# Reordering the start of a graph-network kernel: the first group's third gather, its b pieces and layer 1's bias columns

## The chip, the core and the metric

The kernel runs on one core of a Trainium2 chip. A core has five engines that each work through their own queue of instructions in order: TensorE (PE, matrix products; its weight loads are shown apart as PEld), VectorE (DVE), ScalarE (ACT), GpSimd (POOL) and SyncE (SP, which here only issues DMAs). An instruction that needs the result of another engine waits for a semaphore, and everything behind it in its own queue waits with it. The metric is the device time of one execution in microseconds.

## The reference

Two layers work on 128 graphs of 128 nodes with 64 features. `adj` is a random weighted adjacency matrix; about an eighth of the entries are positive, the first nodes of a graph much more than the last.

```python
# layer 0
mask = (adj > 0.0)
h = relu((x @ W1a)[:, :, None, :] + (x[:, :, None, :] - x[:, None, :, :]) @ W1b + b1)   # 192 wide, per pair j, k
hm = einsum('bjkh,bjk->bjh', h, mask)
x = layernorm(x + hm @ W2 + mask.sum(-1)[..., None] * b2)
# layer 1
m = relu(relu(x @ g_W1 + g_b1) @ g_W2 + g_b2)
msg = relu(adj @ m)
x = layernorm(x + gru(msg @ W_ih.T + b_ih, x @ W_hh.T + b_hh, x))
```

For a pair (j, k) the argument of the relu is u[j] + v[k], with u and v linear in x. The sum over a node's neighbours of relu(u + v) is half of the sum of u + v plus half of the sum of |u + v|. The first half is linear; the kernel gets the second by gathering the v of each node's neighbours, adding u, and summing absolute values.

## The kernel before, in words

The graphs go through in 32 groups of four (`G = 4`). For one group:

- `load`: adjacency, transposed features and features by DMA.
- `masks` (L411, POOL): the mask of all four graphs. `ranks` (L418 PE, L421 ACT) number each node's neighbours; `turned` (L483 PE, L486 ACT) transposes these ranks. `degrees` (L426 PE, L429 and L431 DVE) count neighbours, `counts` (L436 to L446, six small POOL instructions) derive from them how many extra places the nodes need. `offsets` (L453 PE, L456 ACT, L463 and L464 DVE, L470 POOL) and `places` (L500, L504, L507 PE, L510 ACT) lay out those extra places.
- `values0`, `values1` (L527, L530 PE, L534 ACT): u and v of two graphs each. The copy L534 puts them into the tile `uv`. The second matmul (L530) adds bias rows from the tile `three`.
- `pieces`: v is split into three bf16 parts b0, b1, b2, whose sum is v. In group 0 this is done graph by graph: cast (L546 ACT), remainder r (L549 DVE), cast (L552 ACT), remainder (L555 POOL). In later groups it is done for four graphs at once, with r on POOL.
- `picks` (L517, DVE): one-hot matrices, from the ranks (`pick0`, eight) or from the places (`pick1`, four).
- Per graph, four stretches over `pick0` and two over `pick1`. A stretch has a `seed` (L580, ACT: u is copied into a PSUM tile `pv`, of which there are three), a `gather` (L611, PE: 12 matmuls that add the picked b0, b1 and b2) and a `reduce` (L627, DVE: absolute values summed into `part`). The stretches of `pick1` take their u from `us`, which `over` (L591 PE, L598 ACT) computes from `own32`, the output of L470.
- `together`, `sums`, `second` and the rest: the parts are added up and go through layer 1.

The order is written out by hand. Each part is a generator that yields between its steps, and a table gives each step a time; the steps of all groups are sorted by time, and each engine's queue gets its instructions in that order. The times order the steps and do nothing else. Group g's step of time t stands at `g * 768 + t`. Group 0 has a table of its own for its beginning, `FIRST`, with one entry per step; `SETUP` does the same for the preparation of constants. Steps of one time keep the order in which the table names the parts.

```python
for t in SETUP:
    plan.setdefault(t, []).append(run)
...
        if g == 0 and name in FIRST:
            times = FIRST[name] + times[len(FIRST[name]) :]
        run = parts[name]()
        for t in times:
            plan.setdefault(g * PER + t, []).append(run)
...
    for t in sorted(plan):
        for run in plan[t]:
            next(run, None)
```

The last step of `SETUP` prepares layer 1's bias columns on DVE (L242, L243, L245, then L151, L153 or L155 and L160 from `three_rows`, which splits a row of biases into three bf16 rows): 11 instructions that end in the columns of `three` from 256 on. Layer 1 of group 0 reads them first, in L313. The steps around it are group 1's `masks` at 768 - 559 = 209 and its `degrees` at 768 - 402 = 366 and 768 - 367 = 401.

Of the kernel before, what the change touches and what calls it, by code (L numbers as in the profile page):

```python
# [47 lines left out]
}  # L48


SETUP = (-8001, -7999, -7610, -7530, -7400, -7380, -700, -690)
FIRST = {
    "load": (-8000, -7998), "masks": (-7580,), "ranks": (-7520, -7515), "degrees": (-7389, -7388), "counts": (-7387,),
    "offsets": (-7372, -7371, -7366, -7366, -7366, -7366, -7365), "turned": (-7359, -7358),
    "values0": (-7375, -7374, -7370), "values1": (-7368, -7364, -7360), "pieces": (-7373, -7363, -7355, -7350),
    "places": (-7357, -7356), "pick0": (-7512, -7512, -7512, -7512, -7365, -7365, -7365, -7365),
    "pick1": (-7352, -7352, -7351, -7351), "over0": (-7349, -7348), "seed": (-7369, -7366, -7361, -7354),
    "gather": (-7367, -7362, -7354, -7351), "reduce": (-7365, -7358, -7353, -7350),
}


# [18 lines left out]
def adj_resnorm_kernel(  # L80
# [299 lines left out]
    with ExitStack() as fast:  # L380
# [316 lines left out]
        name, g, run = "setup", -1, setup(ps_g, ps_w)  # L697
        for t in SETUP:
            plan.setdefault(t, []).append(run)
# [141 lines left out]
```

## Time and profile before

| what | us |
|---|---|
| median of 3 runs (1056.05 to 1056.41) | 1056.37 |
| the profiled execution | 1053.67 |
| its span | 1051.9 |
| DVE busy | 968.2 |
| PE busy | 952.7 |
| ACT busy | 943.2 |
| POOL busy | 883.3 |

The span runs from the first to the last instruction; the profiled execution's own time is 1.8 us longer. A row of the timeline gives start, duration, engine, line, operation, output and inputs; where the engine was idle just before, brackets give for how long and what ended the wait. In a row with xN, N instructions are merged. The chain of waits goes back from the last instruction, at each step to what released it or to the instruction ahead of it on its engine.

### The profile page before, as it was taken

What the parts mean: (1) busy time and instruction counts of PE and PEld (TensorE: products, weight loads), DVE (VectorE), ACT (ScalarE), POOL (GpSimd) and SP (SyncE); (2) the same over time, 40 slices, a digit from 0 to 9 for tenths busy, and PEclk for the clock granted to TensorE, in tenths of its full rate; (3) what the DMA queues carried; (4) which work ended last, traced back from release to release, by engine and by line L of the source; (5) the groups of instructions that cost most, each with busy time, mean ns of one, the idle gap of its engine ahead of it and who ended that gap; (6) DMA issues with size and microseconds to landing.
All of it is one profiled execution on the core that took longest, in us unless ns stands there. A gap on an engine that the chain in (4) does not pass through costs nothing.

```text
span 1051.9 us, 33435 instructions
## 1 busy us (share of the span) xinstructions
PE 952.7 (91%) x13432; PEld 762.5 (72%) x13432; DVE 968.2 (92%) x2192; ACT 943.2 (90%) x1608; POOL 883.3 (84%) x1291
## 2 busy tenths in 40 slices
PE   6798999999999999999999999999999999999983
PEld 4577777777777777777777777777777877777762
DVE  6888999999999999999999999999999999999971
ACT  4789999999999999999999999999999999999861
POOL 2568788889889888988888898988898888889765
PEclk9799999999999999999999999999999999999995
DMA  4000000000000000000001000000000000000000
GB/s 110 1 22 2 22 22 22 27 27 13 16 27 27 28 27 26 3 27 27 27 27 27 22 7 27 26 27 27 27 4 25 27 27 27 26 7 7 2 7 27
DMA packets 21368, 23.95 MB, mean 23 GB/s; under 512 B 4050, under 2 KB 17112, under 8 KB 21208
## 3 DMA queue, kind: packets, MB, share of 16 engines
q1 hardware_dynamic: 21208, 21.76, 7.1%
q8 instruction: 107, 1.75, 0.7%
q14 instruction: 53, 0.43, 0.1%
HBM read 17.55 MB, written 4.19 MB: 21 GB/s over the span
## 4 chain that ended last, share of the span: by engine, by line
POOL 37%; DVE 29%; ACT 14%; PE 12%; issue 8%; DMA 0%; SPq 0%; POOLq 0%; DVEq 0%; ACTq 0%
DVE part L627 15%; ACT pv L580 7%; POOL part L649 6%; POOL part L653 4%; POOL part L656 4%; PE pv L611 4%; DVE pick L517 4%; POOL r L549 4%; POOL part L651 4%; POOL b L555 3%; DVE own L464 3%; DVE stats L269 2%; POOL yc L279 2%; POOL ua L360 2%; POOL rs L276 2%
## 5 line engine op out<-in xcount | busy, mean ns | idle before, releaser
L627 DVE TENSOR_REDUCE part<-pv 128x192 f32<-128x768 f32 x768 | 699.3, 948 | 32.0 <-PE pv L611 17.5
L611 PE MATMUL pv<-b,pick 64*128 64x192 bf16 x9216 | 501.9, 244 | 39.0 <-ACT pv L580 34.9
L611 PEld LDWEIGHTS <-pick 64*128 64x128 bf16 x9216 | 385.4, 94 | 123.6 <-issue 94.1
L580 ACT COPY pv<-uv 128x768 f32<-128x768 f32 x512 | 407.5, 804 | 16.8 <-DVE part L627 14.5
L580 ACT COPY pv<-us 128x768 f32<-128x768 f32 x256 | 204.6, 817 | 13.2 <-DVE part L627 13.1
L649 POOL TENSOR_TENSOR part<-part 128x384 f32<-128x384 f32 x128 | 127.9, 999 | 19.1 <-DVE part L627 17.3
L534 ACT COPY uv<-pu 128x512 f32<-128x512 f32 x128 | 75.1, 587 | 27.7 <-PE pu L530 23.5
L527 PE MATMUL pu<-wall,xT 64*128 64x512 f32 x256 | 92.0, 637 | 1.6 <-ACT off L456 1.2
L517 DVE TENSOR_SCALAR pick<-rankT 128x512 bf16<-128x512 bf16 x256 | 88.7, 367 | 1.5 <-ACT rankT L421 1.5
L669 PE MATMUL ph<-ownT,part 128*96 128x128 f32 x512 | 87.6, 273 | 0.2 <-POOL part L656 0.2
L470 POOL CAST own<-own 128x512 f32<-128x512 bf16 x32 | 19.6, 611 | 75.2 <-DVE own L464 69.1
L651 POOL TENSOR_TENSOR part<-part 128x192 f32<-128x192 f32 x128 | 77.5, 605 | 5.1
L555 POOL TENSOR_TENSOR b<-r,b 128x1024 bf16<-128x1024 f32 (+1 forms) x35 | 68.9, 1968 | 11.8 <-ACT b L552 8.5
L653 POOL TENSOR_TENSOR part<-part 128x192 f32<-128x192 f32 x128 | 75.9, 593 | 2.6
L591 PE MATMUL pz<-uv,own 128*128 128x192 f32 x256 | 58.6, 352 | 20.4 <-DVE n L352 12.0
L656 POOL TENSOR_TENSOR part<-part 128x192 f32<-128x192 f32 x128 | 75.8, 592 | 0.0
L288 PE MATMUL pw<-w2c,hmT 96*128 96x64 f32 x512 | 75.1, 278 | 0.5 <-ACT hmT L675 0.5
L288 PEld LDWEIGHTS pw<-w2c,hmT 96*128 96x128 f32 x512 | 69.7, 191 | 6.6 <-issue 4.9
L669 PEld LDWEIGHTS ph<-ownT,part 128*96 128x96 f32 x512 | 70.8, 165 | 1.8 <-POOL part L656 0.7
L668 PE MATMUL ph<-ident,part 128*96 128x128 f32 x256 | 71.0, 277 | 0.8 <-POOL part L653 0.6
L276 POOL TENSOR_TENSOR rs<-ve,nhalf 128x4 f32<-128x4 f32 x64 | 66.6, 1040 | 5.3
L549 POOL TENSOR_TENSOR r<-uv,b 128x1024 f32<-128x1024 f32 x31 | 66.1, 2132 | 0.0
(139 smaller groups left out, 1590.9 us busy)
## 6 DMA issues: line engine op xcount, KB each, us to landing
adjT<-in_adjT_dram SPq DMA_DIRECT2D x32, 256.0 KB, 2.8
xT<-in_xT_dram SPq DMA_DIRECT2D x64, 64.0 KB, 2.7
x<-in_x_dram SPq DMA_DIRECT2D x32, 128.0 KB, 2.4
out_dram<-o SPq DMA_DIRECT2D x32, 128.0 KB, 2.1
wab<-in_w_dram SPq DMA_DIRECT2D x2, 96.0 KB, 2.6
bi<-in_b_ih_dram SPq DMA_DIRECT2D x1, 96.0 KB
bias<-in_b_hh_dram SPq DMA_DIRECT2D x1, 96.0 KB
wx<-in_w_hhT_dram SPq DMA_DIRECT2D x2, 48.0 KB, 3.1
```

Of the source, the lines that this page charges most:

```text
L288: nc.tensor.matmul(p[:, i, :], s["hmT"][:, i, c, :], w2c[:, c, :], start=c == 0, stop=False)
L517: nc.vector.tensor_scalar(s[name][:, i], s[src], 2.0 * (first + i) - 1.0, None, ALU.is_equal)
L549: (nc.vector if g == 0 else nc.gpsimd).tensor_tensor(r[:, gs], v, b[0][:, gs], ALU.subtract)
L555: nc.gpsimd.tensor_tensor(b[2][:, gs], r[:, gs], b[1][:, gs], ALU.subtract)
L580: nc.scalar.copy(v, src.rearrange("p (c b h) -> p c b h", c=1, b=1).to_broadcast(list(v.shape)))
L611: nc.tensor.matmul(v[:, h, j, :], pick[ks, a + j, i, :], s[f"b{c}"][ks, i, F : F + H], start=False, stop=c == 2, skip_group_check=True,)
L627: nc.vector.tensor_reduce(into, view(s["pv", i, k]).rearrange("p c b h -> p h c b"), AX.XY, ALU.add, apply_absolute_value=True,)
L649: nc.gpsimd.tensor_tensor(f[:, 0:2], f[:, 0:2], f[:, 2:4], ALU.add)
L651: nc.gpsimd.tensor_tensor(f[:, 0], f[:, 0], f[:, 1], ALU.add)
L653: nc.gpsimd.tensor_tensor(f[:, 0], f[:, 0], f[:, no], ALU.subtract)
L656: nc.gpsimd.tensor_tensor(f[:, 0], f[:, 0], f[:, 1], ALU.add)
L669: nc.tensor.matmul(p[:, i, c, :], s["part1", i0 + i][:, 0, cs], s["ownT"][:, i0 + i, :], start=False, stop=True, skip_group_check=True,)
```

## The change

Only the two tables change. In group 0 the third stretch's seed and gather come ahead of `turned` and `places`; the second, third and fourth graphs' r stand elsewhere among the first reductions, the second ahead of the first reduction; `places`' copy (L510) follows the third graph's b0 and b1; the cast of L470 follows the second graph's b2; the four `pick1` steps lie two ahead of and two behind the fourth reduction and the fourth r. The last step of `SETUP` moves from -690 to 420, which is behind group 1's degrees (401) and ahead of the first stretch over `pick1`'s reduction. Other times are new as well, but give the same order.

```diff
-SETUP = (-8001, -7999, -7610, -7530, -7400, -7380, -700, -690)
+SETUP = (-8001, -7999, -7610, -7530, -7400, -7384, -700, 420)
 FIRST = {
     "load": (-8000, -7998), "masks": (-7580,), "ranks": (-7520, -7515), "degrees": (-7389, -7388), "counts": (-7387,),
-    "offsets": (-7372, -7371, -7366, -7366, -7366, -7366, -7365), "turned": (-7359, -7358),
-    "values0": (-7375, -7374, -7370), "values1": (-7368, -7364, -7360), "pieces": (-7373, -7363, -7355, -7350),
-    "places": (-7357, -7356), "pick0": (-7512, -7512, -7512, -7512, -7365, -7365, -7365, -7365),
-    "pick1": (-7352, -7352, -7351, -7351), "over0": (-7349, -7348), "seed": (-7369, -7366, -7361, -7354),
-    "gather": (-7367, -7362, -7354, -7351), "reduce": (-7365, -7358, -7353, -7350),
+    "pick0": (-7512, -7512, -7512, -7512, -7364, -7363, -7362, -7361), "values0": (-7380, -7379, -7375),
+    "pieces": (-7378, -7359, -7348, -7342), "offsets": (-7377, -7376, -7372, -7371, -7370, -7369, -7358),
+    "seed": (-7374, -7373, -7365, -7354), "values1": (-7368, -7360, -7355), "gather": (-7367, -7366, -7357, -7349),
+    "reduce": (-7356, -7351, -7347, -7343), "turned": (-7353, -7352), "places": (-7350, -7346),
+    "pick1": (-7345, -7344, -7341, -7340), "over0": (-7339, -7338),
 }
```

The queues that result, where they differ (s = seed, g = gather, R = reduction, numbers for graphs or stretches):

```
DVE before: r1  past/own x4  picks  R1  r2  R2  r3  R3  pick1 x4  r4  R4  bias columns  degrees(group 1)
DVE after:  r1  past/own x4  picks  r2  R1  R2  r3  R3  pick1 x2  R4  r4  pick1 x2  degrees(group 1)  bias columns
ACT before: s1 s2 uv b0-2 b1-2 s3 uv rank place b0-3 b1-3 s4 b0-4 b1-4
ACT after:  s1 s2 s3 uv b0-2 b1-2 uv s4 rank b0-3 b1-3 place b0-4 b1-4
PE before:  g1 g2 turned places g3 g4 over
PE after:   g1 g2 g3 turned places g4 over
POOL before: b2-1 own32 b2-2 b2-3 b2-4 mask(group 1)
POOL after:  b2-1 b2-2 own32 b2-3 b2-4 mask(group 1)
```

## The prediction

> **What bounds the kernel now.** First the page's head: the vector engine (DVE) is busy 92%, TensorE (PE) 91%, ScalarE (ACT) 90%, so in the long middle no engine has much room. The change touches only the first 45 us, so I then read the chain of waits and the timeline there, and last the busy time by stretches for the granted clock.
>
> ```profile
> PE 952.7 (91%) x13432; PEld 762.5 (72%) x13432; DVE 968.2 (92%) x2192; ACT 943.2 (90%) x1608; POOL 883.3 (84%) x1291
> ```
>
> The chain of waits (start, length, engine and line), from group 0's third b to the first reductions on group 1's data:
>
> ```profile
> 24.52 0.43 DVE r L549
> 24.95 0.87 DVE part L627
> 25.82 1.07 DVE pick L517 x4
> 26.89 0.34 DVE r L549
> 27.25 0.41 ACT b L552
> 27.74 0.67 POOL b L555
> 28.41 1.61 POOL maskT L411
> 30.33 0.46 PE pc L418
> 30.82 0.59 ACT rankT L421
> 31.40 0.71 ACT pv L580
> 32.16 2.10 PE pv L611 x24
> 34.26 1.76 PE pu L527 x4
> 36.26 0.57 ACT uv L534
> 36.83 0.71 ACT pv L580
> 37.59 0.88 PE pv L611 x12
> ```
>
> The reader is to see that group 1's mask (POOL, L411) is on the chain although its adjacency was loaded long before: it is queued on POOL behind the last graph's third piece (L555), and that behind r and two casts. Whatever makes the fourth b early makes the mask early. The timeline shows the idle time that the change aims at, in brackets, and the DVE's start on the bias columns:
>
> ```profile
> 24.52 0.43 DVE L549 TENSOR_TENSOR r<-uv,b 128x256 f32<-128x256 f32 x1 [2.85 <-ACT b L546]
> 28.20 0.26 DVE L242 COPY bias<-bi 128x64 f32<-128x64 f32 x1
> 37.30 0.96 DVE L627 TENSOR_REDUCE part<-pv 128x192 f32<-128x768 f32 x1 [1.50 <-PE pv L611]
> ```
>
> Busy time by stretches (engine sums, then the granted clock):
>
> ```profile
> 20.00:25.00 5.00, 2.49 (x28) 1.47 (x26) 2.15 (x5) 3.01 (x7) 0.67 (x1) 0.94 0.71 209
> 25.00:30.00 5.00, 2.72 (x16) 1.91 (x15) 4.83 (x12) 2.67 (x6) 2.93 (x3) 0.50 0.01 2
> 30.00:35.00 5.00, 3.55 (x33) 2.65 (x35) 4.39 (x11) 3.83 (x7) 1.59 (x8) 0.50 0.00 0
> 35.00:40.00 5.00, 4.20 (x56) 3.03 (x52) 3.19 (x5) 3.75 (x7) 3.29 (x4) 0.70 0.00 0
> ```
>
> A clock of 0.94 and 0.70 in those stretches puts a half-clock spell from about 24.4 to 38.0 us. In it a gather matmul takes 0.080 us of PE, after it 0.041 (12 of them: 0.67 us with the last one's latency, 1.24 at half clock).
>
> **The change part by part.** Nothing is added or removed: the same instructions stand in another order on PE, DVE, ACT and POOL; the DMA queue keeps its order. So I lay the new order out with each instruction's own duration from the profile. The rows give the hand-overs: r starts 0.03 after the cast it needs (14.64 to 14.67), into POOL it is 0.08 (15.54 to 15.62), into PE 0.05; back to back, the next starts 0.1 (ACT) or 0.08 (DVE) before the row of the one before ends. Old start in brackets.
>
> 1. Third seed and gather ahead. The seed (0.80) runs on ACT at 17.43 to 18.23 in 0.73 us of idle time ahead of the third value's copy, which waits for PE until 18.26 anyway: free. The gather adds 12 x 0.080 = 0.96 on PE ahead of the turned ranks (L483), which move from 20.28 to about 21.2; the rank copy that needs them now comes to its turn on ACT at 21.54, so the cover is ACT's queue with about 0.1 us to spare (beyond it, ACT's order makes the rest of this list later one for one). The first reduction goes behind the second graph's r on DVE.
> 2. Second b. r starts when the picks end, 19.52 [20.39]; b1 on ACT 19.96 [20.84]; first reduction 19.86 [19.53], end 20.80.
> 3. ACT next: fourth value 20.27 [21.88]; fourth seed, which needs the first reduction, 20.84 to 21.64; rank 21.54 [22.36]; third graph's b0 22.02 [24.08], r 22.46 [24.52], b1 22.92; only then place, 23.23 to 23.82 [23.60]. PE has the places' matmuls done by about 22.8, so place waits for ACT alone. Fourth b0 23.72 [26.03].
> 4. DVE: two picks from place at 23.85 (0.55 and 0.28), fourth reduction 24.51, fourth r 25.39 [26.81]. b1 25.83 [27.25], third piece on POOL 26.32 [27.74], mask 26.96 [28.38]. The float copy of own (L470) went behind the second b2 on POOL: 21.1 instead of 18.4; it is needed by the matmuls of L591 after the fourth gather at 23.4, so free. Mask: **1.42 us earlier**.
> 5. With mask, ranks, seeds and gathers keep their spacing: rank cast 29.40 [30.82], first seed 29.88, gather 30.74 [32.16], values L527 32.61 [34.03], copy 34.82 [36.24], seed 35.31 [36.73].
> 6. Bias columns behind the degrees. They took 28.20 to 32.79, 4.59 us, beside the wait for the mask. Now degrees come first, 28.95, and the block runs 29.10 to 33.69. Behind it waits the first reduction of the next stretches: 33.69 [33.41], 0.28 later. Two reductions and a pick bring the reduction that had waited 1.50 us for PE to 36.06 to 37.01 [37.30]: the old 1.50 us of idle time pays for the block. Its readers (message and gates) run near 71 us. What POOL does from the degrees (L436 on) leads by over 3 us and waits for nobody.
> 7. The next stretch's gather starts at 36.17 [37.59], now wholly at half clock: 1.24 instead of the 0.94 that straddled 38.04. Its end leads by 1.42 - 0.30 = 1.12, at 37.41; the reduction at 37.44 finds the DVE free since 37.01. So the DVE has 0.43 us of room, and PE sets the time.
>
> From there the order is the old one, reductions follow each other (41.25 becomes about 40.2), and the loads are far ahead; 31 groups repeat the same order, so the lead is carried to the end. **Sum: -1.42 + 0.30 = about -1.1 us.** Bounds: the DVE's queue caps the gain at 1.1 + 0.43 = 1.5 if PE is faster; contention on the DVE is the price no row settles. A pick takes 0.28 alone and 0.55 to 0.71 beside a POOL instruction, so at most 0.43 for each of the 11 bias instructions that now run beside POOL's counts, sums and mask 2; L151 took 0.33 with POOL busy and idle, and only L245 looked stretched (0.59 for 64 columns, L242 0.26). I take no stretch more than in the old rows; ends 0 and about 1.5 us (three or four hits), of which 0.43 is free.
>
> The profiled execution took 1053.67 us (span 1051.9 and 1.8 around it), the median of the runs is 2.70 above it. So profiled 1052.6, and 1056.37 - 1.1 = **1055.3 us**.
>
> **The clock, and a rule for it.** The half-clock spell lasts 13.65 us, though PE was busy some 85% of 34.6 to 38.0. The Trainium skill (TensorE: Matmul & The Clock Gate, Part 1) has half rate as the default, full rate after about 3.4 us of sustained work and half again after an idle window, the windows running free of the kernel. The drop after PE's gap at 20.9 to 22.5 agrees; the release does not, since one busy window would have ended the spell sooner. By that rule the sum would be -1.4.
>
> **The rivals.**
> - More gain: full clock is back before 36.17. Then the 0.30 is not lost and the DVE's queue sets the end: -1.4 to -1.5, 1054.9 us. For it: the changed order leaves PE idle near 24 to 28.6, so the spell may fall elsewhere. The rule of the clock gate named above speaks for it too. Against: the spell's length in the rows. More than -2.1 needs a mask 0.6 us earlier still; picks that meet no POOL instruction would give 0.3 of that.
> - The change gives nothing: the bias block behind the degrees is stretched by POOL by 1.5 us, or place comes 1 us late and the mask with it; 1.1 - (1.5 - 0.43) leaves 0, 1056.3 us. For it: L245's row and the picks'. Against: the other bias rows.
> - Slower: the clock. If half rate is not left at 38.04 but held for four windows more, to 51.7, ten stretches and a values step lie in it: 10 x 0.47 + 0.87 = 5.6 us. A reduction takes 0.87 per stretch against 0.96 of PE at half rate, so about half is covered: +2.8 - 1.1 = +1.7, 1058.1 us. It decides from about 42 us on. Against: PE is as dense in the new order from 35 us on as before. For it: PE's new idle stretch is 4.7 us long.
>
> **How the numbers follow.** 0.2% of this kernel, 2.1 us, is about what a measurement can tell from no change. Forecast 0.50 (-0.5 to -1.4); more gain 0.24, of which 0.15 beyond -2.1 for what shortens the chain unseen; nothing 0.12 (-0.5 to +0.8); slower 0.14 (+0.8 to +4.5, from half covered to nothing covered), of which 0.10 beyond +2.1. So faster 0.15, within 0.75, slower 0.10. The range runs from -2.4 to +1.0, 1054.0 to 1057.4, and leaves some 0.08 below and 0.12 above; the forecast's own is 1054.9 to 1055.9.
>
> **What would show it.** Right: mask 1 (second L411) near 27.0, degrees before L242 near 29.0, first reduction after the bias block near 33.7, uv L534 of group 1 near 34.8, the idle 1.50 ahead of the reduction at 37.30 nearly gone, everything from 45 us on about 1.1 earlier. Wrong: a mask after 27.5, a bias block over 5.0 us, or a half-clock spell that ends after 42.

## The result: 0.24% faster, about twice the forecast's gain

The changed kernel takes 1051.35 us (median of 14 runs, 1050.59 to 1052.56), the kernel before 1053.77 us (median of 14 runs, 1052.32 to 1056.41). The ratio is 0.9976 [0.9967, 0.9984], which is 2.5 us less (1.7 to 3.5). The forecast was 1.1 us less and 1055.3 us, in a range of 1054.0 to 1057.4. The time lies outside that range for two reasons. One is the base: the three runs that the forecast stood on (1056.05 to 1056.41) were the highest three of the fourteen, and their median lies 2.6 us above the median of all. The other is the gain itself.

The profiled execution took 1052.28 us (span 1050.5) against 1053.67 (1051.9). The busy time of the engines over the whole span is as before: DVE 967.5 us (968.2 before), PE 952.2 (952.7), ACT 943.0 (943.2), POOL 883.4 (883.3).

The chain of waits of the changed kernel (start, length, engine and line), from the fourth graph's r to the copy of group 1's first values (L534):

```profile
25.31 0.34 DVE r L549
...
26.16 0.67 POOL b L555
26.83 1.48 POOL maskT L411
...
30.03 0.41 DVE bias L160
...
30.44 2.10 PE pv L611 x24
32.55 1.76 PE pu L527 x4
...
34.54 0.57 ACT uv L534
```

The chain is the one of before, earlier: r, cast, third piece, mask, and behind it ranks, gather and values. That it now runs through the degrees and the bias columns is a matter of who came last by a hair: the seed (ACT, L580, 29.58 to 30.38) ends within 0.05 us of L160, and the gather of 30.44 needs the seed and reads nothing that L160 writes. The gathers and reductions on this part of the chain are still those of group 0's graphs, first its stretches over `pick1`; of group 1 there are only mask, degrees, ranks and values. Group 0's gathers read none of that; they wait because they, or their seeds, are queued behind it.

The timeline of the changed kernel, with the rows that answer to those of before:

```profile
26.80 1.50 POOL L411 TENSOR_SCALAR maskT<-adjT 128x512 bf16<-128x512 f32 x1
...
28.65 0.17 DVE L429 TENSOR_REDUCE deg<-pd 128x4 f32<-128x8 f32 x1 [2.60 <-PE pd L426]
...
28.81 0.18 DVE L242 COPY bias<-bi 128x64 f32<-128x64 f32 x1
...
31.82 1.01 DVE L151 CAST piece<-bias 128x320 bf16<-128x320 f32 x1
33.58 1.81 DVE L627 TENSOR_REDUCE part<-pv 128x192 f32<-128x768 f32 x2
35.66 2.82 DVE L627 TENSOR_REDUCE part<-pv 128x192 f32<-128x768 f32 x3
35.87 1.40 PE L611 MATMUL pv<-b,pick 64*128 64x192 bf16 x24 [0.65 <-ACT pv L580]
```

The mask starts at 26.80 (28.38 before), the degrees at 28.65 (32.71), the rank cast at 29.10 (30.82), the next stretches' reductions at 35.66 with no idle time ahead, where DVE had idled for 1.50 us until 37.30. At 45 us everything is 1.9 us earlier. Of that, 0.13 us was there before the change can act: group 0's own rank cast (L421) starts at 7.33 in this execution and at 7.46 in that of before. Net of the start the lead is 1.77. It is not carried to the end unchanged: from group to group the cast L494 starts between 1.48 and 2.13 us earlier than before (1.90 in group 0, 2.13 in the last).

And the busy time by stretches (engine sums, then the granted clock):

```profile
25.00:30.00 5.00, 0.71 (x5) 0.31 (x6) 2.33 (x12) 2.03 (x5) 2.99 (x5) 0.80 0.01 2
30.00:35.00 5.00, 4.56 (x42) 3.35 (x42) 4.86 (x9) 3.40 (x7) 4.69 (x8) 0.52 0.00 0
```

PE is left with 0.71 us of work from 25 to 30 (2.72 before), as the prediction said. The clock did not do what was forecast: it was full until 28.0, and half only from 28.0 to 34.83, instead of 24.39 to 38.04.

### The profile page after: what moved, and what is told of

Same layout as the page of the kernel before. It is cut to its first block, busy times and chain, and to the rows that moved or that the text cites. A ratio compares the mean times of both kernels' runs of the same rounds, so it can differ in the third digit from the quotient of the medians.

```text
span 1050.5 us, 33434 instructions
## 1 busy us (share of the span) xinstructions
PE 952.2 (91%) x13432; PEld 762.4 (73%) x13432; DVE 967.5 (92%) x2192; ACT 943.0 (90%) x1608; POOL 883.4 (84%) x1291
## 3 DMA queue, kind: packets, MB, share of 16 engines
q8 instruction: 107, 1.75, 0.7%
## 4 chain that ended last, share of the span: by engine, by line
PE 31%; POOL 21%; DVE 20%; ACT 20%; issue 7%; SPq 0%; DMA 0%; DVEq 0%; POOLq 0%; ACTq 0%
PE pv L611 12%; ACT pv L580 10%; DVE part L627 10%; PE ph L669 3%; PE pu L527 3%; POOL part L649 3%; ACT uv L534 3%; POOL rs L276 2%; DVE stats L269 2%; ACT b L546 2%; POOL part L653 2%; POOL yc L279 2%; POOL part L656 2%; DVE pick L517 2%; PE ph L668 2%
## 5 line engine op out<-in xcount | busy, mean ns | idle before, releaser
L580 ACT COPY pv<-uv 128x768 f32<-128x768 f32 x512 | 407.5, 804 | 16.6 <-DVE part L627 14.2
L580 ACT COPY pv<-us 128x768 f32<-128x768 f32 x256 | 204.7, 817 | 13.1 <-DVE part L627 13.1
L649 POOL TENSOR_TENSOR part<-part 128x384 f32<-128x384 f32 x128 | 128.0, 1000 | 19.6 <-DVE part L627 17.9
L534 ACT COPY uv<-pu 128x512 f32<-128x512 f32 x128 | 75.1, 587 | 27.0 <-PE pu L530 22.8
L470 POOL CAST own<-own 128x512 f32<-128x512 bf16 x32 | 19.5, 610 | 74.0 <-DVE own L464 68.0
L591 PE MATMUL pz<-uv,own 128*128 128x192 f32 x256 | 57.9, 349 | 20.4 <-DVE n L352 12.4
```

The source lines that it names most:

```text
L534: nc.scalar.copy(uv[:, 2 * h + i, :], ps[h])
L580: nc.scalar.copy(v, src.rearrange("p (c b h) -> p c b h", c=1, b=1).to_broadcast(list(v.shape)))
L649: nc.gpsimd.tensor_tensor(f[:, 0:2], f[:, 0:2], f[:, 2:4], ALU.add)
```

## The experiments

Each kernel was run against the kernel before on the same chip; in the eleven experiments the runs of before have medians of 1053.09 to 1053.57 (1053.77 in the first row). "Lead" is how much earlier group 0's cast L494 (45.78 us in the trace of before; with fillers the same instruction) starts in the one profiled execution, less the shift of group 0's first rank cast (7.46).

| kernel | median us | ratio to before | lead us |
|---|---|---|---|
| changed | 1051.35 | 0.9976 [0.9967, 0.9984] | 1.77 |
| changed, again (e_after2) | 1051.34 | 0.9979 [0.9970, 0.9988] | 1.80 |
| order alone (e_order) | 1051.46 | 0.9981 [0.9972, 0.9990] | 2.07 |
| bias move alone (e_bias) | 1053.63 | 1.0004 [0.9995, 1.0013] | 0.26 |
| third gather back (n_third) | 1052.45 | 0.9991 [0.9981, 1.0002] | 0.74 |
| second r back (n_r2) | 1051.87 | 0.9986 [0.9974, 0.9998] | 1.74 |
| changed + fillers (f_after) | 1051.42 | 0.9978 [0.9968, 0.9988] | 2.25 |
| order + fillers (f_order) | 1050.69 | 0.9965 [0.9951, 0.9980] | 2.12 |
| before + early mask (m_before) | 1053.42 | 0.9999 [0.9990, 1.0008] | 0.36 |
| order + early mask (m_order) | 1049.81 | 0.9965 [0.9953, 0.9977] | 4.28 |
| changed + early mask (m_after) | 1049.50 | 0.9960 [0.9947, 0.9974] | 4.06 |
| the same + fillers (f_m) | 1049.67 | 0.9962 [0.9948, 0.9975] | 4.69 |

The theory is that of the prediction: the new order makes the fourth b early, POOL's queue hands that on to group 1's mask, and the bias columns are paid for by the DVE's idle time. One rival says that the bias move itself gives the time; another that the clock does, by a half-clock spell that falls elsewhere; a third that the 0.24% is no more than the spread of runs.

### The changed kernel again

> The changed kernel once more, timed on the same chip as the kernel before and as its parts. The queue theory (group 1's mask comes earlier because the fourth b does, and nothing else moves the end) gives -1.4 to -1.9 us against the kernel before: 1.42 from the order, up to 0.5 from where the half-clock spell falls. If the -2.4 us measured over all chips so far is the whole effect on every chip, it is -2.4 here too. In the profile: mask 1 between 26.7 and 27.0, a half-clock spell that begins at the end of the 3.41 us window that lies in PE's idle time from 24.2 to 28.3.

Measured: 0.9979 [0.9970, 0.9988], so the gain is there a second time, on other runs of both. In this execution the clock was full from 19.41 instead of 21.17 and half from 26.23 to 36.47 instead of 28.00 to 34.83, and still the lead is the same. Where the spell falls differs from execution to execution of one kernel, and moves single steps by some 0.3 us: the last 34 matmuls of the first three gathers took 2.32 us here against 3.25, and the next stretches' first gather lay at half clock up to 36.47, so that its reduction had to wait.

### The order alone, the bias move alone

The order alone (the tables of the changed kernel, the last step of the preparation where it was):

```diff
-SETUP = (-8001, -7999, -7610, -7530, -7400, -7384, -700, 420)
+SETUP = (-8001, -7999, -7610, -7530, -7400, -7384, -700, -690)
```

> The new order of group 0 alone; the bias columns stay at -690, ahead of group 1's degrees. Queue theory: mask 1 is as early as in the full change (26.9), so the gain is that of the full change or slightly more, -1.1 to -2 us, since the bias block then runs from about 26.1 to 30.7 in time in which DVE waits, and the first reduction behind it starts near 31.7 in place of 33.6. Rival theory (the gain comes from the bias block being out of the way of the degrees and of what follows them): no gain, within 0.4 us of the kernel before.

The bias move alone (in the kernel before):

```diff
-SETUP = (-8001, -7999, -7610, -7530, -7400, -7380, -700, -690)
+SETUP = (-8001, -7999, -7610, -7530, -7400, -7380, -700, 420)
```

> The move of the bias columns alone; group 0 keeps its old order. Queue theory: the mask stays at 28.4, degrees at 30.3, the bias block from 30.5 to 35.1, the reduction behind it 1.7 us later than before, which the 1.5 to 1.9 us of idle DVE time behind it just pays for: 0 us, between -0.3 and +0.5. Rival theory (the bias move is where the gain is): -1.5 to -2.5 us.

Measured: the order alone gives 0.9981, all of the gain; the bias move alone gives 1.0004, nothing. The rival of the bias columns falls. In the old order the move puts the first reduction behind the block 1.79 us later, and nothing follows from it, which the timeline of the bias move alone shows:

```profile
35.20 1.81 DVE L627 TENSOR_REDUCE part<-pv 128x192 f32<-128x768 f32 x2
...
37.28 0.94 DVE L627 TENSOR_REDUCE part<-pv 128x192 f32<-128x768 f32 x1
```

The third reduction of this stretch starts at 37.28, as before (37.30), now without the idle 1.50 us. That is step 6 of the prediction, seen alone. With the order alone DVE idles instead:

```profile
34.83 0.96 DVE L627 TENSOR_REDUCE part<-pv 128x192 f32<-128x768 f32 x1 [0.79 <-ACT uv L534]
36.38 1.82 DVE L627 TENSOR_REDUCE part<-pv 128x192 f32<-128x768 f32 x2 [0.58 <-ACT pv L580]
```

The idle time here is 0.79 + 0.58 = 1.37 us: it is the room that the bias columns fill in the changed kernel, at no gain and no loss that the ratios show. The lead of the order alone is 0.3 longer, but its `place` (L510) also came earlier, at 22.95 instead of 23.26: its second and third gathers met full clock from 20.31 us, 0.86 before those of the changed kernel.

### Which part of the order

The third stretch's seed and gather back behind the places:

```diff
-    "seed": (-7374, -7373, -7365, -7354), ... "gather": (-7367, -7366, -7357, -7349),
+    "seed": (-7374, -7373, -7354.9, -7354), ... "gather": (-7367, -7366, -7349.5, -7349),
```

> The changed kernel with the third stretch's seed and gather back behind the places' matmuls; all else as changed. Queue theory: PE is then idle while it waits for the fourth value's copy and the rank copy, gather 3 and 4 run one after the other behind the places, the fourth reduction, the fourth r and so the mask come about 1.0 us later than in the changed kernel (mask near 27.9): 0.6 to 1.2 us slower than the changed kernel, -0.5 to -1.3 against the kernel before. If the third stretch does nothing by itself: as the changed kernel, -1.9.

The first reduction back ahead of the second graph's r:

```diff
-    "reduce": (-7356, -7351, -7347, -7343),
+    "reduce": (-7359.5, -7351, -7347, -7343),
```

> The changed kernel with the first reduction ahead of the second graph's r again; all else as changed. Queue theory: the second b1 on ACT waits 0.8 us longer for r, ACT's queue carries this to the fourth b, mask near 27.6: 0.6 to 0.9 us slower than the changed kernel, -1.0 to -1.3 against the kernel before. If the gather ahead is the whole of it: as the changed kernel, -1.9.

Measured: without the third gather ahead the lead falls from 1.8 to 0.74 and the ratio to 0.9991, whose interval includes 1. The timeline of that kernel shows the place: the third reduction waits for PE, and the fourth reduction and the fourth r are queued behind it.

```profile
24.23 0.96 DVE L627 TENSOR_REDUCE part<-pv 128x192 f32<-128x768 f32 x1 [1.34 <-PE pv L611]
...
26.37 0.41 DVE L549 TENSOR_TENSOR r<-uv,b 128x256 f32<-128x256 f32 x1
```

In the changed kernel the third reduction starts at 22.83 and this r at 25.24: having the third gather ahead is worth 1.13 us to it, 1.02 net of the start. Part of it can be the clock's: in this execution half clock returned from 22.00 to 25.42, so the third and fourth gathers took 2.10 us together, where the changed kernel's fourth took 0.67 alone. By an estimate from these figures, at full clock the third reduction would have started some 0.46 us earlier. The medians say the same as the lead: 1.1 us more than the changed kernel on the same chip (1052.45 against 1051.34), though the intervals of the two ratios still overlap.

With the first reduction ahead of the second r, that r starts at 19.79 instead of 19.19, and of these 0.60 only 0.19 reach the mask (26.99 against 26.80, and an expected 27.6): ACT, which in the changed kernel idles for 0.24 us ahead of the turned ranks' copy (L486, 21.56), takes up most of the rest. That idle time goes with the first gathers at half clock until 21.17: in the second execution of the changed kernel, at full clock from 19.41, ACT has none there. The execution with the first reduction ahead had full clock from 18.95 to 22.36; against that second one its mask is 0.51 us later, net of the start. Then the clock gives this back. It was full again from 25.78 to 29.19, so the matmul of the ranks (L418) took 0.38 us instead of 0.59, and the rank cast starts at 29.08, as in the changed kernel (29.10). So the second r's place is worth 0.2 to 0.5 us to the mask, by where the clock falls; the ratio, 0.9986, can't tell it from nothing. The other moves of the new order (`place` behind the third graph's pieces, `pick1` in two halves, the cast of L470 later) were not taken back one by one.

### The clock

Matmuls that nobody reads, behind those of L591, fill PE's hole, once in the changed kernel and once with the order alone:

```diff
+                if g == 0 and i0 == 0:
+                    q = ps_w.tile([N, 512], F32, tag="w", name="fill")
+                    for _ in range(14):
+                        nc.tensor.matmul(q, ones_h, zeros, start=True, stop=True)
```

> The changed kernel with 14 matmuls more on PE behind the fourth gather and L591 (ones by zeros, 512 columns, into a PSUM tile that nobody reads), in the 4.1 us in which PE waits for the mask; the output is the same. It fills the window in which the clock falls to half rate. Clock theory: no half-clock spell before 45 us. The seeds of the next stretches still start near 29.6, the gathers behind them take 1.2 in place of 2.1 us and L527 0.9 in place of 1.8, but DVE is held by the bias block until 33.5 and its next three reductions cannot end before 36.5, so little comes of it: 0 to -0.3 us against the changed kernel, -1.9 to -2.2 against the kernel before. If the clock were what holds the changed kernel: 1.5 us faster than the changed kernel.

> The same 14 matmuls in the kernel that has the new order alone, with the bias columns ahead of the degrees. There DVE is free from about 31.5 on, so PE's rate sets the time: with no half-clock spell the next reductions lead by 1.3 to 2 us more, -3.2 to -3.9 us against the kernel before. Rival (DVE or ACT sets the end here too): as the order alone, -1.9.

Measured: neither rid the kernel of the spell; both shortened it to one window (29.69 to 33.10 and 31.33 to 34.74). The changed kernel with fillers takes the time of the changed kernel (0.9978), though its lead is 0.5 longer. With the order alone the ratio is 0.9965, against 0.9981 without fillers. Its 3.7 us lie in what was expected, but the medians differ by 2.4 us alone, the intervals overlap, and the lead (2.12 against 2.07) shows none of it. By the leads, a spell of one window instead of two is worth at most half a microsecond here; a kernel without any spell was not seen. Whether the rest of that ratio comes from the fillers stays open.

### Group 1's mask early

If the mask's place in POOL's queue is what carries the gain, more is to be had by taking it out from behind the third pieces. Group 1's load goes to just ahead of group 0's work and its mask behind the first graph's third piece:

```diff
+EARLY = {"load": (-7600,), "masks": (-7366,)}
...
-                if g == 0 and name in FIRST:
-                    times = FIRST[name] + times[len(FIRST[name]) :]
+                times = FIRST[name] + times[len(FIRST[name]) :] if g == 0 and name in FIRST else times
+                times = tuple(t - PER for t in EARLY[name]) if g == 1 and name in EARLY else times
```

> The changed kernel with group 1's load and mask at earlier times: the mask goes into POOL's queue right behind the first graph's third piece, near 16.3 us, where POOL is idle; the DMA queue keeps its order. Queue theory: the mask no longer waits for the fourth b, degrees and ranks follow the fourth gather at once (degrees near 26), the seeds of the next stretches start near 27.6 in place of 29.6, and the end is 2 to 2.5 us earlier than in the changed kernel, -3.5 us against the kernel before. Rival theory (the mask's place on the chain is only apparent, DVE's queue sets the end): within 0.5 us of the changed kernel.

> The kernel before with group 1's load and mask at earlier times, as in the version that was 3.8 us faster, but with the old order of group 0 and the bias columns ahead of the degrees. If the mask alone were the limit, this alone gives the 2 us that it gave on top of the change. Queue theory: here the fourth b on ACT and the fourth reduction stand in front of the same seeds (the copy of us follows the fourth b1 in ACT's queue), so mask and seeds lead by only 0.7 us: -0.4 to -1.2 against the kernel before, more where the clock comes back early.

> New order of group 0, group 1's mask early, bias columns ahead of the degrees. Queue theory: the bias block starts near 25.7 either way, degrees follow it near 30.4; PE's ranks matmul shares a PSUM ring with the degrees, so the ranks wait a little less or more, and the end is as with the bias columns behind the degrees within 0.5 us: -3.3 to -4.2 against the kernel before.

Measured: on the new order the early mask brings 0.9960 (with the bias columns behind the degrees) and 0.9965 (ahead of them), in medians 3.8 us in both, about what was expected; the mask starts at 16.30 and 15.54. On the old order it brings nothing, 0.9999, where 0.4 to 1.2 us were expected. The chains of waits show why. First the changed kernel with the early mask:

```profile
25.67 0.41 ACT b L552
26.07 0.38 ACT us L598
...
26.81 0.48 ACT rankT L421
```

The mask is off the chain, and ACT's queue sets the rank cast, which starts at 26.71 in the timeline, against 29.10. Then the kernel before with the early mask:

```profile
26.77 1.15 PE pv L611 x12
27.91 1.59 PE pz L591 x4
29.53 0.49 ACT us L598
...
30.06 0.60 PE pc L418
...
30.68 0.59 ACT rankT L421
```

Here the rank cast waits for the ranks' matmul (L418), that for the copy `us` on ACT, which empties a PSUM tile of the same pool, the copy for PE's products of L591, and these for the fourth gather, which the old order seeds at 25.92. This chain ends at a rank cast of 30.68, 0.14 us ahead of the one that waits for the mask (30.82), so it takes over at once. Part of this the early mask did itself. It ran on POOL at 16.29 to 17.78 beside L463 and L464 on DVE: one L464 took 0.64 us instead of 0.35, and the first reduction came at 19.92 instead of 19.53. With half clock back at 23.58 instead of 24.39 as well, the copy `us` came at 29.53 instead of 28.90. With the copy at 28.90 and the same spacing the rank cast would stand at 30.05, 0.77 us ahead, which is the 0.7 that was expected; that is an estimate. On the new order an L464 is stretched as much (0.64), but this does not show at the turned ranks' copy (L486), which starts at 21.56 with and without the early mask. There the fourth gather is done by 23.4 us, so the order removes the wait for `us` together with the mask's. That is why the early mask is worth something there only.

With eight fillers of the kind above in the changed kernel with the early mask:

> The version with the early mask and the bias columns behind the degrees, with 8 matmuls more on PE behind L591, ones by zeros, 512 columns, 1.7 us at full rate, into a PSUM tile that nobody reads; the output is the same. PE then idles about 2 us less between the fourth gather and the next ones. Clock theory: a half-clock spell is shorter or absent before 40 us, but DVE is held by the bias block until 31.3, so at most 0.7 us comes of it; and where the extra matmuls run at half rate (3.4 us) they push the degrees back by up to 1 us: -3.3 to -4.7 against the kernel before.

Measured: 0.9962 against 0.9960, no difference, with the spell shortened to one window (29.00 to 32.41). The changed kernel with the early mask, at 1049.50 us, has the lowest median of all; its variants (1049.67 and 1049.81) can't be told from it.

## Why the prediction was wrong: the base and the clock, not the mask

**Steps 1 to 4, the mask 1.42 earlier: right.** It came 1.58 earlier, 1.45 net of the earlier start; the fourth r, forecast at 25.39, started at 25.24. Small errors cancel in it. The first picks met no POOL instruction and took 0.90 us instead of 1.31, so the second r started at 19.19 (forecast 19.52); but ACT then waited 0.24 us for PE ahead of the turned ranks' copy, where step 1 had 0.1 us to spare. So `place` (L510) started at 23.26, which net of the start is 0.16 later than the forecast 23.23, and the first two picks behind it took 0.50 (23.87 to 24.37) where the prediction gave them 0.66. What the steps did not say is which of the moves carries it. By the runs the third gather does, with about 1.0 of the 1.8 us of lead; step 1 priced what it costs (nothing) and no step what it brings.

**Step 5, fixed spacing: 0.14 short.** The mask took 1.50 us instead of 1.64. Before, it ran beside the bias columns on DVE; now DVE is idle then. The parts show it: with the bias move alone the mask took 1.50, with the order alone, beside the bias columns, 1.58. The rank cast leads by 1.72. The prediction calls the reductions at the end of its chain the first on group 1's data; they are group 0's, as said above, and its sums do not depend on it. This is the other side of the contention that step 6 counted: the move takes DVE work away from beside the mask as well as putting it beside the counts.

**Step 6, the bias columns: right.** The block took 4.84 us (28.81 to 33.65) instead of 4.59; one L151 took 1.01 beside the POOL sum L649 instead of 0.33, and L245 0.19 beside a small POOL instruction (L436, 128x4) instead of 0.59 beside the mask. The first reduction came at 33.58 (forecast 33.69) and the idle 1.50 is gone. The DVE's room was undercounted. Behind the block the two reductions took 1.81 (1.92 before) and the pick 0.42 (0.55), and the reduction behind them started at 35.66, where the prediction had 36.06. So the cap of 1.5 that the prediction set on the gain was 0.4 short, and the lead went past it.

**Step 7 failed: "now wholly at half clock", +0.30.** The gather of 35.87 ran at full clock, and took 0.20 off the chain where 0.30 was to be added. The step rested on the sentence that the rule of the clock gate does not hold for the release, "since one busy window would have ended the spell sooner". Cut at the clock's own steps, the trace of before says otherwise. Busy time by stretches of 3.41 us, before:

```profile
31.22:34.63 3.41, 2.47 (x26) 2.29 (x27) 2.87 (x8) 3.41 (x7) 1.21 (x6) 0.50 0.00 0
34.63:38.04 3.41, 3.02 (x25) 1.75 (x23) 1.91 (x3) 1.81 (x4) 3.33 (x5) 0.50 0.00 0
38.04:41.46 3.42, 2.69 (x52) 2.09 (x47) 3.08 (x8) 3.21 (x7) 0.33 (x1) 1.00 0.00 0
```

And of the changed kernel:

```profile
24.59:28.00 3.41, 0.00 (x0) 0.00 (x0) 1.46 (x4) 1.14 (x3) 1.84 (x2) 1.00 0.03 6
28.00:31.41 3.41, 1.68 (x19) 1.27 (x21) 2.62 (x11) 2.31 (x5) 2.33 (x8) 0.50 0.00 0
31.41:34.83 3.42, 3.42 (x29) 2.21 (x26) 3.35 (x5) 1.82 (x5) 3.34 (x4) 0.50 0.00 0
34.83:38.24 3.41, 2.29 (x46) 1.80 (x42) 3.36 (x5) 3.41 (x7) 0.76 (x2) 1.00 0.00 0
```

The first number behind the length is PE's busy time. Before, the windows at half clock were busy 49% and 52% (24.39 to 31.22, not shown), 72% and 88%, and the spell ends with the 88%: that was the first busy window, not one of several. After, an empty window at full clock drops it, and a window of 100% ends it, two windows later. The Trainium skill (TensorE: Matmul & The Clock Gate, Part 1) has half rate again after an idle window and full rate after one of sustained work. The end of the spell agrees with it in both traces; the drop agrees in the changed kernel (0% busy), while in the kernel before it came behind a window that was busy 47%, which is not idle. The sum that the prediction gave by that rule, -1.4, was nearer than its own -1.1.

**The sum.** Net of the start: 1.45 (mask) + 0.14 (its length) + 0.20 (clock) = 1.79, which is the lead of 1.77 but for rounding; forecast 1.42 - 0.30 = 1.12. The term of the gain that was mis-sized most is the clock's, by 0.50, then contention, 0.14. In the median the gain is 2.5 us (1.7 to 3.5) and 2.2 (1.3 to 3.2) the second time; the lead of 1.8 lies within both. What of the difference is real is not shown. Single executions tell little here, since late clock windows move them. In the changed kernel's profile the clock of the last group drops at 1021.28 (before: 1024.49), and of the 2.13 us at the last L494 (start included) 1.30 arrive at POOL's last instructions; in its second profile one window of half clock at 999.03 to 1002.44 takes 1.4 us (1.75 at the L494 ahead of it, 0.33 at the next). In that second execution the sum is another one with the same result: the mask 1.77 net of the start, since the first gathers met full clock sooner, its length 0.14, and the next gather 0.10 against it, together 1.81 for a lead of 1.80.

**The rivals.** "More gain" was the case that came, at a chance of 0.24. In the profile taken it came by its own mechanism, the clock back (34.83) before 36.17; its price of -1.4 to -1.5 was too low by the cap above. In the second execution the clock was back only at 36.47, and the lead was as long, so the lead does not hang on that alone. "Nothing" fell with step 6. "Slower" fell: at the start of the thirteen traces no spell ends after 38.04, that of the kernel before.

**The base failed too, and by more.** Of the 3.95 us between the forecast 1055.3 and the measured 1051.35, the base makes up 2.60. The gain makes up the other 1.35, of which the terms above show 0.65; the remainder is open. The profile shown took 1053.67 us and the three runs 1056.05 to 1056.41. The prediction saw the 2.7 us between them and hung its time on the three runs. With 1053.77 as the base its own sum gives 1052.7, 1.3 us above the measured time, and its range from -2.4 to +1.0 would be 1051.4 to 1054.8, whose lower end the time just misses. Such runs of the kernel before came again in the experiments (2 of 27 and 6 of 31 above 1055.7 us). Why they take so long is open; no run here tells.

## What to carry to other kernels

When a step early in a kernel is to come sooner, look for what is queued next behind it on each engine it passes: freeing the mask gave some 2 us on the new order and nothing on the old, where a chain over PE and a copy on ACT let the rank cast start only 0.14 us sooner. Work put into an engine's idle time costs nothing, and brings nothing, as long as another engine ends that wait. And before a clock term goes into a sum, cut the profile at the clock's own steps, and ask how busy each window was; when the runs at hand and the profiled execution disagree, the base is the largest uncertainty of the forecast.

## What the runs showed of the hardware

Between 15 and 50 us all thirteen traces (before, changed and the eleven experiments) show the clock of TensorE changing in steps of 3.41 us. Spells of half clock are one to four such windows long. Each of them ends with a window in which PE was busy 88% to 100%; windows at half clock that were busy 21% to 86% did not end one. The windows at full clock that were followed by a drop were busy 0% to 51%. But PE's busy share is no threshold. Elsewhere a window at half clock that was busy 91% (8.35 to 11.76 without the third gather ahead) or 92% (1029.10 to 1032.52 in the last run with fillers) did not end its spell, and in the changed kernel a window at full clock that was busy 48% (82.60 to 86.01) was not followed by a drop. What the clock goes by is not shown here. The windows' phase differs between executions: 1.76 us between two of the same kernel, full from 21.17 and from 19.41.
